# Four edits to a hybrid scan, attention and FFN kernel: an FFN input turned by DMA, norms that share a power, earlier group norms, a fifth C product on GpSimd

## The chip, the cores and the metric

The kernel runs on one NeuronCore of a Trainium2 chip. The core has five engines with an instruction queue each, worked through in order: TensorE (PE in the profile: matrix products and transposes into PSUM), VectorE (DVE), ScalarE (ACT), GpSimd (POOL), and SyncE (SP), which here only issues DMAs. They meet through semaphores. The metric is the device time of one execution in microseconds (us).

## The reference, cut to what matters

```
# layer 0, on x of (4, 64, 64, 96); L = 4096 positions, C = 96 channels, S = 16 states
xn   = layernorm(groupnorm(x), eps=1e-3) * gamma + beta
proj = xn @ W_in + b_in
value, gate, delta = proj[..., :C], sigmoid(proj[..., C:2*C]), proj[..., 2*C:3*C]
A, Bm, Cm = the rest of proj, each (B, L, C, S)
def step(h, ins):
    h_new = d * (A_t * h) + d * (B_t * u_t)
    y = g_t * sum(C_t * h_new, axis=-1)
x = x + scan(step) @ W_out + b_out
# layer 1
t = t + attention(layernorm(t, 1e-5))      # linear: q (k^T v), six heads, no softmax
t = t + ffn(layernorm(t, 1e-5))            # 96 -> 384 -> 96, inputs rounded to fp8 (5 exponent,
                                           # 2 mantissa bits), sums rounded to fp16, relu
```

The group norm has 32 groups of 3 channels and takes its mean and variance over all 4096 positions of an image.

## The kernel before

**Tiles.** Each of the 4 images is cut into 8 chunks of 512 positions, 32 chunks in all. A chunk has `NT` = 12 steps, one for each pair of a quarter of the states (4 of 16) and a third of the channels (32 of 96): 128 partitions by 512 positions. There are `K` = 384 steps.

**One step.** TensorE makes three products B, A and C, each of three matmuls over split fp32 operands (`project`, line 265). ScalarE copies B to SBUF with its bias (`b_copy`), GpSimd multiplies it by d*u (`b_mul`), VectorE multiplies A by d (`a_mul`), scans along the positions (`scan`) and multiplies C by the state (`c_mul`). In the steps whose number within the chunk is in `ON_POOL`, ScalarE copies C instead (`c_copy`) and GpSimd multiplies it (`c_mul_pool`). PSUM has two banks for A, one for B, two for C (C and D in turn) and three, M, for all the rest.

**Order.** The main loop (lines 1426 to 1448) writes the instructions step by step: in step s the B product of step s+3, the A product of s+1, the C product of s, then GpSimd's and VectorE's parts, then `call(s)`, which adds all else that is due in this step. Each engine has its own queue, so this is the order of each queue, not a time. What is due when stands in the table `AT`: a step number relative to the first step of the chunk (for the front), to the same step (for the tail of the layer 0 work), or to eight chunks later (for the FFN). So a number modulo 12 tells where in a chunk the work stands. The last steps of the FFN of image 3, and all that falls behind step 384, are ordered by the planner `Plan`.

**The front** of a chunk (class `Front`, line 681): `load_x`; group norm applied by GpSimd (`centre`, `scale`); statistics by VectorE, `rstd` by GpSimd (add eps, power -0.5, mean times -1, times r), `apply` by ScalarE; four transposes by TensorE; then d and u: `d_out` (ScalarE), `du_out` (VectorE), `write` to DRAM (`ddd`), and `read`: four DMAs that bring d and d*u back on four times as many partitions (`rep`, 1.5 MB together). `b_mul` and `a_mul` of the chunk read `rep`.

**The group norm** of an image needs sums over its 8 chunks: `load_gx` brings a chunk of x into `gx` (one buffer), TensorE transposes it (`sums`), ScalarE sums values and squares (`sums_out`). Before, the sums of image b+1 are made while image b runs, one per chunk, except that image 1's come every seven steps in image 0.

**The FFN** of a chunk (function `ffn`, line 1081): `fetch` (`xal`), `attention`, residual, statistics, `rstd`, `apply` (which writes fp8), then `transpose` (four matmuls with an identity into PSUM) and `quant_in` (ScalarE, PSUM to fp8 in SBUF: `xq`), three products `hidden0` to `hidden2`, each with three ScalarE passes, `project_f`, and the store.

**The y of a chunk** is summed over the state quarters: three DMAs by GpSimd's queue add the C products of quarters 1 to 3 to those of quarter 0 (`gather`, 768 KB each), and TensorE folds the rest.

All DMAs but the gathers and a few loads at the start come from SyncE's queue, which also works in order: a DMA that waits for its source keeps those behind it waiting.

Of the kernel before, what the change touches and what calls it, by code (L numbers as in the profile page):

```python
# [17 lines left out]
P = 128  # L18
# [22 lines left out]

    "load_x": -39, "centre": -25, "scale": -24, "stats": -22, "rstd": -22, "apply": -21,
    "transpose": -14, "affine": -13, "upper": -13, "low": -12, "proj_d": -9, "d_out": -9,
    "proj_u": -9, "du_out": -9, "write": -9, "read": -6, "proj_gate": -3, "gate_out": -1,

    "gather1": 7, "gather2": 11, "gather3": 14,

    "state_sum": 18, "gated": 18, "project_out": 19, "residual": 19, "stats_a": 20,
    "rstd_a": 21, "apply_a": 22, "transpose_a": 33, "keep": 34, "spill": 39, "gram": 24,
    "gram_out": 24, "gram_add": 26,  # L50

    "fetch": 21, "attention": 26, "residual_f": 26, "stats_f": 26, "rstd_f": 27, "apply_f": 29,
    "transpose_f": 30, "quant_in": 31, "hidden0": 37, "relu0": 37, "hidden1": 31, "relu1": 33,
    "hidden2": 38, "relu2": 38, "project_f": 40, "round_out": 40, "bias_out": 40, "total": 46,
    "store": 51,

    "sums": -31, "sums_out": -30,
}
ON_POOL = (0, 2, 7, 8)
XBUFS = 15  # L60


@with_exitstack
def conv_attn_hybrid_kernel(
# [130 lines left out]
    mhalf = const.tile([P, J], F32, name="mhalf")  # L195
    nc.gpsimd.memset(mhalf, -0.5)

# [13 lines left out]
    for r in range(2):  # L211
        t = const.tile([P, J, CA], F32, tag=f"xa{r}", name=f"xa{r}")
        nc.gpsimd.memset(t[:, :, C:CA], 1.0)
        xa_t.append(t)
        t = const.tile([CA, J, P], F32, tag=f"xal{r}", name=f"xal{r}")
        nc.gpsimd.memset(t[C:CA], 1.0)
        xal_t.append(t)

        t = const.tile([P, J, P], F8, tag=f"xn8{r}", name=f"xn8{r}")
        nc.gpsimd.memset(t, 0.0)  # L220
        xn8_t.append(t)
# [141 lines left out]

    class LayerNorm:


        def __init__(self, eps, nm):
            self.eps, self.nm, self.r = eps, nm, None

        def stats(self, src):  # L370
            st = small.tile([P, J, 6], F32, tag="st", name=f"st_{self.nm}")
            self.mv = small.tile([P, J, 2], F32, tag="mv", name=f"mv_{self.nm}")
# [5 lines left out]
        def rstd(self, shift=True):  # L378

            self.r = small.tile([P, J], F32, tag="rstd", name=f"rstd_{self.nm}")  # L380
            nc.gpsimd.tensor_scalar(self.r, self.mv[:, :, 1], self.eps, None, ALU.add)
            self.root()
            if not shift:
                return
            self.nmr = small.tile([P, J], F32, tag="nmr", name=f"nmr_{self.nm}")
            nc.gpsimd.tensor_scalar(self.nmr, self.mv[:, :, 0], -1.0, None, ALU.mult)
            nc.gpsimd.tensor_tensor(self.nmr, self.nmr, self.r, ALU.mult)

        def offset(self):

            self.r = small.tile([P, J], F32, tag="rstd", name=f"rstd_{self.nm}")
            nc.vector.tensor_scalar(self.r, self.mv[:, :, 1], self.eps, None, ALU.add)

        def root(self):
            nc.gpsimd.tensor_tensor(self.r, self.r, mhalf, ALU.pow)
# [140 lines left out]
    class GroupNorm:  # L536
# [82 lines left out]
        def root(self):  # L619
            nc.gpsimd.tensor_tensor(self.m[:, 1:2], self.v, mhalf[0:C, 0:1], ALU.pow)  # L620
# [21 lines left out]
        def spread_out(self, k0=0, k1=2):  # L642
            if k0 == 0:
                t = self.t = small.tile([P, 2, C], F32, tag="gmr", name=f"gmr_{self.b}", bufs=2)
# [3 lines left out]
    def group_norm(b, s0):  # L648
        q = {}

        def make():
            q["g"] = GroupNorm(b)
            q["g"].first()

        def call(name, *args):
            getattr(q["g"], name)(*args)

        when = [s0 + AT["sums"] + NT * n for n in range(NCH)]  # L660
        if b == 1:
            when = [8, 15, 22, 29, 36, 43, 50, 57]
        if b > 1:
            at(when[0] - 7, load_gx, b, 0)
        at(when[0] - 2, make)
        for n in range(NCH):
            if n:
                at(max(when[n] - 7, when[n - 1]), load_gx, b, n)
            at(when[n], call, "sums", n)
            at(when[n] + AT["sums_out"] - AT["sums"], call, "sums_out", n)  # L670
# [4 lines left out]
        for n, args in enumerate(chain):  # L675
            at(when[-1] + AT["sums_out"] - AT["sums"] + 1 + n, call, *args)

# [3 lines left out]
    class Front:  # L681
# [3 lines left out]
        def __init__(self, b, i):  # L685
            self.b, self.i, self.nm = b, i, f"{b}_{i}"
            self.ln = LayerNorm(1e-3, f"c_{self.nm}")
# [95 lines left out]

    def front(b, i, s0, f=None):
        if f is None:
            f = Front(b, i)
# [13 lines left out]
        late = {"centre": 0, "scale": 0, "stats": 1, "rstd": 2, "apply": 3}  # L800
# [115 lines left out]
    end.tries = 1500  # L916
# [12 lines left out]
    def tail(b, i):  # L929
# [4 lines left out]
        v, ln = {}, LayerNorm(1e-5, f"a_{nm}")  # L934
# [146 lines left out]
    def ffn(b, i, s0):  # L1081
        nm = f"{b}_{i}"
        v, ln = {}, LayerNorm(1e-5, f"f_{nm}")
# [21 lines left out]
        def apply():  # L1105

            v["xn"] = next_of(xn8_t, "xn8")
            (ln.apply_vector if vector else ln.apply)(v["xn"], t, saturate=False)

        def transpose():  # L1110
            ps = v["ps"] = bank("C" if phase["end"] else "M", [P, TC], f"xq_ps_{nm}")
# [6 lines left out]
        def quant_in():  # L1118
            v["xq"] = tile_of("xq", "h", [C, TC], F8, "xq")
# [59 lines left out]
        def store():  # L1179
# [8 lines left out]
            (("transpose_f", transpose), ("quant_in", quant_in)),  # L1188
# [17 lines left out]
        if apply in done and transpose not in done:  # L1206
# [289 lines left out]
```

## Time and profile before

| | us |
|---|---|
| median of 3 runs (1180.49 to 1182.14) | 1182.05 |
| span of the profiled execution | 1179.2 |
| TensorE busy, of the span | 1138.6 (97%) |
| VectorE busy | 1113.3 (94%) |
| GpSimd busy | 1040.1 (88%) |
| ScalarE busy | 812.9 (69%) |
| the chunks' first scans: image 0 begins | 34.8 |
| image 1 begins | 297.9 |
| the last chunk begins | 1073.3 |

The profile is of one execution, whose span lies 2.85 us below the median of the runs. TensorE's busy time is that of overlapping matmuls, whose ends are modelled: a busy TensorE isn't one at its peak. What the engines wait for is told by the rows of waits; where an engine isn't the bottleneck, its waits cost nothing. A few rows of the costliest groups (columns: line, engine, operation, output and inputs, shapes, count; then busy us, mean ns of one; then idle us before them and what ended most of it) name the operations that the change touches:

```profile
L395 POOL TENSOR_TENSOR rstd_c<-rstd_c,mhalf 128x4 f32<-128x4 f32 x32 | 33.8, 1055 | 6.5 <-DVE rstd_c L392 3.9
L386 POOL TENSOR_SCALAR nmr_c<-mv_c 128x4 f32<-128x4 f32 x31 | 7.4, 239 | 0.0
L885 POOL TENSOR_TENSOR ch<-ch,h 128x512 f32<-128x512 f32 x126 | 169.8, 1347 | 7.0 <-ACT ch L882 3.3
L876 DVE SCALAR_TENSOR_TENSOR ch<-Dps,b_bac,h 128x512 f32<-128x512 f32 x160 | 118.6, 741 | 0.4
L1120 ACT ACTIVATE xq<-xq_ps 96x512 fp8e5<-96x512 f32 x32 | 18.9, 590 | 3.6 <-PE xq_ps L1113 3.6
```

### The profile page before, as it was taken

How to read it: one execution, taken by the hardware profiler on the slowest of the kernel's cores; microseconds unless marked ns; L12 is line 12 of the kernel's file. 1: busy time of each engine (PE TensorE's matmuls, PEld its weight loads, DVE VectorE, ACT ScalarE, POOL GpSimd, SP SyncE). 2: the span in 40 equal slices, each digit the busy share in tenths (PEclk: the TensorE clock that was granted, in tenths of full speed). 3: DMA queues.
4: the chain of work that ended last, by engine and by line, in shares of the span. 5: the costliest groups of instructions: out<-in, count | busy, mean ns of one | idle time of the engine just before them, and what ended most of it. 6: DMA issues, size and time to landing. Idle time of an engine off the chain costs nothing. (4 is left out here: it accounts for less than half of the span.)

```text
span 1179.2 us, 19184 instructions
## 1 busy us (share of the span) xinstructions
PE 1138.6 (97%) x5882; PEld 874.2 (74%) x5882; DVE 1113.3 (94%) x2079; ACT 812.9 (69%) x1833; POOL 1040.1 (88%) x1187
## 2 busy tenths in 40 slices
PE   6999999999999999999999999999999999999885
PEld 5777776777777777777777777777777777777563
DVE  6999999999999999999999999999999999999865
ACT  4666655655556777777777778777777777776475
POOL 5798888888889999999999999999999999988575
PEclk8999999999999999999999999999999999999987
DMA  7676776778876777778766776776777768766221
GB/s 184 141 165 145 169 153 156 161 163 178 177 161 148 154 162 166 163 164 191 162 160 151 170 174 159 173 165 156 156 159 159 174 155 182 159 134 146 67 65 51
DMA packets 104288, 182.12 MB, mean 154 GB/s; under 512 B 42637, under 2 KB 50769, under 8 KB 104186
## 3 DMA queue, kind: packets, MB, share of 16 engines
q1 hardware_dynamic: 90060, 106.96, 37.6%
q0 software_dynamic: 13536, 73.93, 31.4%
q8 instruction: 46, 0.75, 0.3%
q14 instruction: 56, 0.46, 0.1%
q10 hardware_dynamic: 590, 0.02, 0.0%
HBM read 69.12 MB, written 24.77 MB: 80 GB/s over the span
## 5 line engine op out<-in xcount | busy, mean ns | idle before, releaser
L836 POOL TENSOR_TENSOR bu<-bu,rep 128x512 f32<-128x512 f32 x384 | 511.9, 1343 | 42.7 <-ACT state L862 32.8
L852 DVE TENSOR_TENSOR_SCAN h<-Aps,state,bu 128x512 f32<-128x512 f32 x336 | 425.9, 1268 | 0.3 <-issue 0.2
L833 ACT ACTIVATE bu<-Bps,b_bac 128x512 f32<-128x512 f32 x384 | 262.8, 684 | 198.8 <-PE Bps L269 193.1
L845 DVE SCALAR_TENSOR_TENSOR Aps<-Aps,b_bac,rep 128x512 f32<-128x512 f32 x384 | 281.6, 733 | 4.7 <-PE Aps L269 4.3
L269 PE MATMUL Bps<-xs,w 128*128 128x512 f32 x768 | 267.1, 429 | 3.8 <-ACT bu L833 3.1
L269 PE MATMUL Aps<-xs,w 128*128 128x512 f32 x768 | 241.8, 396 | 1.2 <-DVE h L852 1.0
L885 POOL TENSOR_TENSOR ch<-ch,h 128x512 f32<-128x512 f32 x126 | 169.8, 1347 | 7.0 <-ACT ch L882 3.3
L269 PEld LDWEIGHTS Aps<-xs,w 128*128 128x128 f32 x768 | 143.9, 188 | 36.9 <-DVE h L852 2.7
L269 PEld LDWEIGHTS Bps<-xs,w 128*128 128x128 f32 x768 | 126.6, 190 | 45.8 <-ACT gx_ps L577 12.6
L269 PE MATMUL Aps<-xl,w 128*128 128x512 f32 x384 | 151.8, 395 | 0.0
L269 PE MATMUL Bps<-xl,w 128*128 128x512 f32 x384 | 151.5, 395 | 0.0
L269 PE MATMUL Dps<-xs,w 128*128 128x512 f32 x384 | 120.7, 395 | 0.0
L269 PE MATMUL Cps<-xs,w 128*128 128x512 f32 x384 | 120.6, 395 | 0.0
L876 DVE SCALAR_TENSOR_TENSOR ch<-Dps,b_bac,h 128x512 f32<-128x512 f32 x160 | 118.6, 741 | 0.4
L891 POOL DMA_DIRECT2D ch<-ch x94 | 88.9, 946 | 1.4 <-DMA ch<-ch 1.1
L269 PEld LDWEIGHTS Bps<-xl,w 128*128 128x128 f32 x384 | 72.3, 188 | 17.5
L269 PEld LDWEIGHTS Aps<-xl,w 128*128 128x128 f32 x384 | 72.1, 188 | 17.6
L269 PEld LDWEIGHTS Dps<-xs,w 128*128 128x128 f32 x384 | 72.1, 188 | 17.5
L269 PEld LDWEIGHTS Cps<-xs,w 128*128 128x128 f32 x384 | 72.1, 188 | 17.5
L882 ACT ACTIVATE ch<-Cps,b_bac 128x512 f32<-128x512 f32 x94 | 64.5, 686 | 24.2 <-PE Cps L269 24.2
L269 PE MATMUL Cps<-xl,w 128*128 128x512 f32 x192 | 75.8, 395 | 0.0
L269 PE MATMUL Dps<-xl,w 128*128 128x512 f32 x192 | 75.6, 394 | 0.0
(200 smaller groups left out, 2049.4 us busy)
## 6 DMA issues: line engine op xcount, KB each, us to landing
ch<-ch POOLq DMA_DIRECT2D x94, 768.0 KB, 6.7
rep<-ddd SPq DMA_DIRECT2D x124, 384.0 KB, 7.5
ddd<-dd SPq DMA_DIRECT2D x31, 384.0 KB, 3.2
xl<-lo SPq DMA_DIRECT2D x62, 128.0 KB, 2.4
x<-in_x_dram SPq DMA_DIRECT2D x32, 192.0 KB, 2.9
xatd<-xat SPq DMA_DIRECT2D x32, 192.0 KB, 3.6
xal<-xatd SPq DMA_DIRECT2D x32, 192.0 KB, 5.4
out_dram<-o SPq DMA_DIRECT2D x32, 192.0 KB, 2.5
```

Source lines behind the costliest of these rows:

```text
L269: nc.tensor.matmul(ps, lhsT=wt[:, n], rhs=mv, start=(n == 0), stop=(n == 2))
L833: nc.scalar.activation(self.bu, self.b_ps, AF.Identity, bias=self.bias(0))
L836: nc.gpsimd.tensor_tensor(self.bu, self.bu, rep[self.b, self.i][:, 1, self.cg], ALU.mult)
L845: nc.vector.scalar_tensor_tensor(self.a_ps, self.a_ps, self.bias(1), rep[self.b, self.i][:, 0, self.cg], ALU.add, ALU.mult,)
L852: nc.vector.tensor_tensor_scan(self.h, self.a_ps, self.bu, 0.0 if self.i == 0 else state[self.sh, self.cg], ALU.mult, ALU.add,)
L876: nc.vector.scalar_tensor_tensor(self.slot(), self.c_ps, self.bias(2), self.h, ALU.add, ALU.mult)
L882: nc.scalar.activation(self.ch, self.c_ps, AF.Identity, bias=self.bias(2))
L885: nc.gpsimd.tensor_tensor(self.ch, self.ch, self.h, ALU.mult)
L891: nc.gpsimd.dma_start(chs[g, 0], chs.pop((g, sh)), accum_op=ALU.add)
```

## The change

Four edits and a new table of steps:

- **The FFN's input** is turned by a DMA in 22 of 32 chunks. `apply` writes its fp8 values into the high byte of 2-byte cells (`xn8` is now fp16, 128 by 4 by 128), SyncE issues a transposing DMA of these cells into `xq`, and the `hidden` products read `xq` as fp16, in which such a cell has the same value. The four transposing matmuls and `quant_in` stay only in the ten chunks that the planner orders at the end.
- **Norms share a power.** Norms due in the same step put their means and variances into one tile (class `Roots`), and GpSimd takes power -0.5 of all at once. In the new table the convolution's norm (step -19) and the FFN's (29) fall on the same step of a chunk; the attention's (21) stays alone. The adds and the multiplication by -1 become tensor-tensor operations with constant tiles.
- **All group norms early.** The sums of images 1, 2 and 3 are made in steps 8 to 107, at steps given by `GN_AT`, and `gx` is loaded up to four steps ahead.
- **`ON_POOL`** has five steps instead of four.

```diff
 AT = {
-    "load_x": -39, "centre": -25, "scale": -24, "stats": -22, "rstd": -22, "apply": -21,
-    "transpose": -14, "affine": -13, "upper": -13, "low": -12, "proj_d": -9, "d_out": -9,
-    "proj_u": -9, "du_out": -9, "write": -9, "read": -6, "proj_gate": -3, "gate_out": -1,
-    "gather1": 7, "gather2": 11, "gather3": 14,
...
-    "fetch": 21, "attention": 26, "residual_f": 26, "stats_f": 26, "rstd_f": 27, "apply_f": 29,
-    "transpose_f": 30, "quant_in": 31, "hidden0": 37, "relu0": 37, "hidden1": 31, "relu1": 33,
-    "hidden2": 38, "relu2": 38, "project_f": 40, "round_out": 40, "bias_out": 40, "total": 46,
-    "store": 51,
+    "load_x": -33, "centre": -25, "scale": -24, "stats": -20, "rstd": -19, "apply": -18,
+    "transpose": -14, "affine": -13, "upper": -13, "low": -13, "proj_d": -9, "d_out": -9,
+    "proj_u": -8, "du_out": -7, "write": -7, "read": -7, "proj_gate": -4, "gate_out": -4,
+    "gather1": 6, "gather2": 10, "gather3": 13, "state_sum": 18, "gated": 18, "project_out": 19,
+    "residual": 19, "stats_a": 20, "rstd_a": 21, "apply_a": 22, "transpose_a": 34, "keep": 35,
+    "spill": 35, "gram": 24, "gram_out": 25, "gram_add": 28, "fetch": 19, "attention": 24,
+    "residual_f": 24, "stats_f": 27, "rstd_f": 29, "apply_f": 31, "turn_f": 31, "hidden0": 34,
+    "relu0": 37, "hidden1": 33, "relu1": 33, "hidden2": 38, "relu2": 41, "project_f": 42,
+    "round_out": 43, "bias_out": 47, "total": 50, "store": 55, "sums": -31, "sums_out": -30,
 }
-ON_POOL = (0, 2, 7, 8)
+GN_AT = {
+    1: [8, 16, 23, 29, 36, 41, 47, 57],
+    2: [12, 20, 27, 31, 39, 43, 53, 59],
+    3: [65, 68, 76, 80, 90, 95, 100, 107],
+}
+GX_AHEAD = 4
+ON_POOL = (0, 2, 3, 5, 8)
...
-        t = const.tile([P, J, P], F8, tag=f"xn8{r}", name=f"xn8{r}")
+        t = const.tile([P, J, P], F16, tag=f"xn8{r}", name=f"xn8{r}")
...
+    class Roots:
+        def root(self):
+            if self.done:
+                return
+            self.done = True
...
+                nc.gpsimd.tensor_tensor(
+                    self.r[:, k:m], self.mv[:, k:m, :, 1], eps_t[ln.eps][:, 0 : m - k], ALU.add
+                )
+            nc.gpsimd.tensor_tensor(self.r, self.r, mhalf[:, 0:n], ALU.pow)
+            nc.gpsimd.tensor_tensor(self.nmr, self.mv[:, :, :, 0], minus[:, 0:n], ALU.mult)
+            nc.gpsimd.tensor_tensor(self.nmr, self.nmr, self.r, ALU.mult)
...
+        order = sorted((s, b, n) for b, steps_of in place.items() for n, s in enumerate(steps_of))
+        for k, (s, b, n) in enumerate(order):
+            if k:
+                at(max(s - GX_AHEAD, order[k - 1][0]), load_gx, b, n)
+            if n == 0:
+                at(s - 2, make, b)
+            at(s, call, b, "sums", n)
+            at(s + 1, call, b, "sums_out", n)
...
-            (ln.apply_vector if vector else ln.apply)(v["xn"], t, saturate=False)
+            cells = v["xn"].bitcast(F8).rearrange("p j (c k) -> p j c k", k=2)[:, :, :, 1]
+            (ln.apply_vector if vector else ln.apply)(cells, t, saturate=False)
+
+        def turn():
+            v["xq"] = sb("xq", [P, J, P], F16, f"xq_{nm}")
+            nc.sync.dma_start(
+                v["xq"], v["xn"].rearrange("p j c -> p (j c)"), transpose=True
+            )
+            v["xq"] = v["xq"][0:C].rearrange("c j p -> c (j p)")
...
-            (("transpose_f", transpose), ("quant_in", quant_in)),
+            (("turn_f", turn),),
```

In the queues this gives, per chunk of images 1 to 3, on SyncE: `x`, `ddd`, four `rep`, the store of an output, the transposing DMA, `xal`, three copies of the split, `xatd`. Before it was `ddd`, the store, `xatd`, four `rep`, `x`, `xal`, `gx`, three copies.

## The prediction

> **What bounds the kernel now.** I read the page's slices first, then busy time by stage, then VectorE's timeline over one chunk, then SyncE's timeline with the DMA share, because one part of the change adds a transfer that TensorE waits for. Busy time by stage (columns: stretch, its us, each engine's busy us, granted clock, DMA share, GB/s):
>
> ```profile
> 34.80:297.90 263.10, 257.66 (x1220) 197.77 (x1219) 255.57 (x422) 157.78 (x377) 229.16 (x243) 1.00 0.72 158
> 297.90:1073.30 775.40, 774.98 (x4024) 598.01 (x4023) 757.38 (x1400) 575.62 (x1306) 721.36 (x816) 1.00 0.74 163
> 1104.30:1179.20 74.90, 53.83 (x382) 38.09 (x373) 45.80 (x156) 45.48 (x93) 45.52 (x63) 0.84 0.21 59
> ```
>
> The first row is image 0 (8 chunks, 32.9 us each), the second the 23 chunks from image 1's start to the last chunk's (33.7 us each), the third the tail, which the change hardly touches. TensorE, VectorE and GpSimd are all above 93% in the second; ScalarE, at 74%, has room. VectorE in image 3:
>
> ```profile
> 804.83 1.28 DVE L852 TENSOR_TENSOR_SCAN h<-Aps,state,bu 128x512 f32<-128x512 f32 x1
> 806.02 0.74 DVE L845 SCALAR_TENSOR_TENSOR Aps<-Aps,b_bac,rep 128x512 f32<-128x512 f32 x1
> ...
> 809.10 0.73 DVE L876 SCALAR_TENSOR_TENSOR ch<-Dps,b_bac,h 128x512 f32<-128x512 f32 x1
> 809.76 1.27 DVE L852 TENSOR_TENSOR_SCAN h<-Aps,state,bu 128x512 f32<-128x512 f32 x1
> ```
>
> No idle time stands in it, and start follows start: 1.19 us for a scan, 0.66 for a product. The next chunk's first scan starts at 838.22, 33.4 us later, so VectorE's order sets the pace. TensorE is close behind: in the timeline a block of three products takes 0.70 us (Aps starts at 503.74, Cps at 504.44), three blocks 2.1 us a step, 25.2 us a chunk. Start to start in the same view the small ones add, per chunk: the d, u and gate products 2.1, the state sum 1.0, output and attention 0.8 each, gram 0.6, two transposes 0.7, the FFN 1.3 (of it 0.3 for transposing its input): 7.3. TensorE's own work is about 32.5 us. Neither engine can lose much.
>
> SyncE's queue around the replication of d and d*u:
>
> ```profile
> 578.91 0.32 SPq L769 DMA_DIRECT2D ddd<-dd  x1
> 579.27 0.45 SPq L1180 DMA_DIRECT2D out_dram<-o  x1
> 579.77 0.90 SPq L961 DMA_DIRECT2D xatd<-xat  x1
> 582.22 1.75 SPq L776 DMA_DIRECT2D rep<-ddd  x4
> ...
> 584.00:586.00 2.00, 2.00 (x15) 0.89 (x13) 2.00 (x3) 1.80 (x6) 2.00 (x3) 1.00 1.05 257
> 586.00:588.00 2.00, 2.00 (x11) 1.49 (x9) 1.82 (x3) 0.79 (x3) 1.76 (x3) 1.00 1.07 221
> 588.00:590.00 2.00, 2.00 (x14) 1.64 (x13) 1.03 (x3) 1.15 (x2) 1.89 (x2) 1.00 1.10 223
> ```
>
> `rep` waits 3.3 us for `ddd` to land, and then its 1.5 MB fill all 16 DMA engines until about 590. What is issued behind it waits:
>
> ```profile
> 248.48 2.51 SPq L776 DMA_DIRECT2D rep<-ddd  x4
> 251.03 0.44 SPq L125 DMA_DIRECT2D x<-in_x_dram  x1
> 251.57 1.15 SPq L130 DMA_DIRECT2D gx<-in_x_dram  x1
> ...
> DMA to landing us min/median/max: 4.8/7.2/11.4
> ```
>
> The maximum is this `gx`: 192 KB took 11.4 us to land, against 2.9 us for an `x` load of the same size on a quiet queue.
>
> [...] No run here shows one; I price its 128 KB at 225 GB/s (windows above), 0.6 us, as an estimate.
>
> **The change part by part.**
>
> *Five C products on GpSimd.* VectorE loses one 0.66 us product per chunk: 33.4 becomes 32.8 us. ScalarE gains a copy of 0.69 us and loses `quant_in` (0.59): even. GpSimd gains 1.25 us (start to start of its products).
>
> *One power for two norms.* Of three chains add, power, times -1, times r, two (convolution and FFN norm, both at step 5 modulo 12) merge. A chain costs 0.24+1.05+0.24+0.20 = 1.7 us and about 1.87 with gaps, three 5.6. An 8-column power isn't in the trace. Below: as 4 columns, 1.05; above: twice, 2.1. The one-column power (651 ns for 96x1) and four columns (1050) give 0.13 us a column, so I take 1.6. The chains then cost about 4.2 us, and GpSimd ends at -0.15 us per chunk (between -0.7 and +0.35). It stays under 32.8.
>
> *Group norms in the first image.* 16 sums (four 128x128 transposes each, about 0.36 us of TensorE; 1.6 us of ScalarE) leave images 1 and 2 for image 0, where no FFN runs. TensorE there has 2.2 us less work per chunk than later, so 0.7 us more fits, and ScalarE is at 60%. Loads of `gx` four steps ahead mostly avoid the time of `rep`. Worth up to 0.5 us in 16 chunks where TensorE is nearly the bound; image 0, with its lost product, I put at -2 us in all.
>
> *The transposing DMA.* It removes four FFN transposes (0.3 us of TensorE) and `quant_in`, in 22 chunks; the ten in the tail keep them. The hidden products now stream fp16 instead of fp8, which the trace doesn't have; with the same 512 columns I give them the same time (if they took as long as three of the split products, 0.2 us each more, TensorE would lose 0.6 us a chunk). It adds a wait: `hidden1`, on TensorE at step 33, waits for a DMA issued at step 31, and behind `hidden1` stand all of TensorE's products. In SyncE's new order it comes after `ddd`, the four `rep` and an output store. And `du_out` moves from step 3 to 5 modulo 12, so `rep` goes two steps later: just ahead of the transpose.
>
> Count from T0, the end of `du_out`, which is the start of scan 6 (583.7 in the chunk shown). `rep` is issued at T0+3.3, its fourth 1.3 us later, and with the page's median of 7.5 us to landing it lands at T0+12.1. The store (192 KB) and the transpose (128 KB) follow, 1.4 us at the same rate: T0+13.5. The first gather also moves, from step 7 to 6, and will share the engines with `rep`; I add 0.8 us (0 if it doesn't, 3 if all its 768 KB go first). The transpose lands at about T0+14.3.
>
> TensorE reaches `hidden1` in the middle of step 9 (its other per-chunk products stand half a step behind VectorE in the same way: the gram's copy, of step 24, that is 0, runs at 0.9 in the trace). Step 6 is on VectorE a scan, a product with A, one with C and the gating (1.19+0.64+0.66+0.6), step 7 the same with the residual for the gating, step 8 a scan, a product with A and the statistics (2.8); with half of step 9 that makes 3.1+3.0+2.8+1.2, so T0+10.1. It stands for 4 us, and behind it the blocks B, A and C of the next steps. ScalarE waits with it (the copies of `relu1` need `h_ps`), and VectorE as soon as it has used up A, of which two banks exist. From `hidden1` to the next `du_out`, TensorE has seven steps of 2.1 us, 1.4 us of the eighth and 3.9 us of small products (two transposes 0.7, gram 0.6, attention 0.8, two hidden products 0.3, d and u 1.4), 20.0 in all; then VectorE has a product with A and `du_out` itself, 1.3. That is 21.3, so the period becomes 14.3+21.3 = 35.6 us, against 33.7: of the 4 us, 1.2 go into VectorE's lost product and TensorE's lead, and the FFN transposes that are gone. Break-even is a landing at T0+12.4. Nothing makes the loss good later in the chunk: TensorE, with 32.2 us of work, has no idle time to catch up in.
>
> *`rep` itself later.* GpSimd's first product with it starts at 595.99, 12.3 us after 583.7, about when it lands (T0+12.1). That product ends some 3.2 us before its scan (597.3 against 600.5). A delay below this costs nothing alone; in the forecast it lies beside TensorE's stall.
>
> *Sum.* 21 periods with the stall, 1.9 us each: +40. Image 0: -2; the two chunks of image 1 before the first stall: -1.5. The span goes from 1179.2 to 1215.7. The median of the runs is 2.85 above the span; I keep this: 1218.5 us. A measurement tells about 0.2%, 2.4 us, from no change.
>
> **Rivals.**
>
> *The transpose lands in time.* [...] against: the 11.4 us. Then VectorE's 32.8 us rule from image 1 on: 23 chunks times 0.9 is -21, with image 0 -23: 1159 us. This is the case on the other side, decided by a landing before about T0+11.5; from T0+12.4 the stall eats the gain.
>
> *It breaks even.* A landing near T0+12.5 gives 33.8 us: about 1180. It asks for 1.8 us less than I count: with no gather in the way (0.8), and another 1 us saved on store or transpose.
>
> *The gather goes ahead of `rep`.* With 3 us instead of 0.8, the landing is at T0+16.5, the period 37.8, the sum 21 times 4.1 less 3.5: +83, 1264 us. For it: the gather's earlier step. Against: it waits for products of the steps before, and in the chunk shown goes out at 586.85, after `rep`.
>
> *The shared power costs more than it saves.* At the upper bound GpSimd needs some 32.3 us, still under VectorE's 32.8. It moves nothing by itself.
>
> **How the numbers follow.** The forecast's own case, 1195 to 1235, has 0.48; in time or nearly (1150 to 1179) 0.29; break-even (within 0.2%) 0.04; between it and 1195, 0.05; above 1235, 0.14. So faster 0.29, same 0.04, slower 0.67. The range that leaves out no more than 2 in 10 runs from 1157 to 1252. The likeliest case alone: 1195 to 1235.
>
> **What would show it.** Right: a wait of `h_ps` on TensorE for the DMA of `xq`, 3 to 5 us, some 21 times; `xq`'s median to landing above 7 us; steps 9 and 10 of a chunk longer than before, with VectorE idle before a product with `Aps`; VectorE's busy share falling from 94%. Wrong: `xq` lands within 5 us of its issue, or TensorE shows no such wait; then the period is about 32.8 us. If in image 0 TensorE waits for `gx`, the step of the group norms was wrong. An 8-column power near 2.1 us, or GpSimd without idle time, would show the third step wrong.

## The result, and the profile after

| | before | after |
|---|---|---|
| median, us | 1182.05 (1180.49 to 1183.79) | 1381.60 (1376.86 to 1392.44) |
| ratio to before, 95% interval | | 1.169 (1.165 to 1.174) |
| span of the profiled execution, us | 1179.2 | 1390.7 |
| image 0, first scan to first scan of image 1 | 263.0 | 283.2 |
| chunks 8 and 9 | 64.4 | 74.0 |
| 21 periods, chunk 10 to the last | 711.1 (33.9 each) | 893.3 (42.5 each) |
| from the last chunk's first scan to the end | 105.9 | 105.2 |

The profile after is of the slowest of the five runs, 10.8 us above their median, so its stages add up to more than the medians differ by. Its span is 211.5 us longer than before: 182.3 of them in the 21 periods in which a transposed input is used, 20.2 in image 0, where no FFN runs, and 9.6 in the two chunks between.

The page of the kernel after says it in its head (busy time and share of each engine) and in the chain that ended last, where a DMA now stands with 6% of the span; the last two lines are the `rep` of the pages before and after, from the lists of DMA issues:

```profile
PE 1184.8 (85%) x5797; PEld 913.1 (66%) x5797; DVE 1111.9 (80%) x2049; ACT 817.9 (59%) x1841; POOL 1055.8 (76%) x1166
...
PE 19%; DMA 6%; DVE 2%; POOL 1%; ACT 1%; issue 1%; SPq 0%; DVEq 0%; ACTq 0%; POOLq 0%
...
rep<-ddd SPq DMA_DIRECT2D x124, 384.0 KB, 7.5
rep<-ddd SPq DMA_DIRECT2D x124, 384.0 KB, 9.7
```

Busy times of VectorE and GpSimd are within 2% of those before; it is idle time that was added. TensorE's busy time grew by 46 us with 85 matmuls fewer; why is told below. The median `rep` takes 9.7 us from issue to landing, against 7.5. The list of waits (us in total, times, longest):

```profile
DVE Aps L883 <- PE Aps L275: 200.6, 57, 9.0
ACT h L1178 <- PE h_ps L1170: 169.9, 21, 9.0
...
PE h_ps L1170 <- DMA xq<-xn: 153.3, 21, 8.1
POOL bu L874 <- DMA rep<-ddd: 102.1, 27, 5.2
```

The line of `xq` is the cause of the first two: 21 times TensorE stood at `hidden1`, 7.3 us on average, and VectorE and ScalarE stood for TensorE. One of them, from the start of SyncE's queue to the end of the stand. SyncE's issues (start, us, operation):

```profile
578.34 0.32 SPq L806 DMA_DIRECT2D ddd<-dd  x1
581.40 1.82 SPq L813 DMA_DIRECT2D rep<-ddd  x4
583.27 1.86 SPq L1226 DMA_DIRECT2D out_dram<-o  x1
585.24 3.77 SPq L1151 DMA_TRANSPOSE xq<-xn  x1
```

the gather that GpSimd issues, from its own timeline:

```profile
581.38 0.92 POOL L929 DMA_DIRECT2D ch<-ch  x1 [0.30 <-POOL ch L923]
```

and TensorE's timeline at `hidden1`:

```profile
587.98 0.39 PE L275 MATMUL Dps<-xl,w 128*128 128x512 f32 x1
596.21 0.59 PE L1170 MATMUL h_ps<-xq,w_q 96*128 96x512 f16 x1 [7.84 <-DMA xq<-xn]
596.24 1.41 PE L275 MATMUL Bps<-xs,w 128*128 128x512 f32 x2
597.45 0.63 PE L275 MATMUL Bps<-xl,w 128*128 128x512 f32 x1
```

T0, the end of `du_out`, is 578.3. The gather (768 KB) is issued 0.02 us before `rep` and shares the engines with it: in the packet records its packets run from 584 to 590, and `rep`'s last packet ends at 594.4, 13.0 us after the issue (before, 7.6 in the chunk that the prediction shows). The store and the transpose behind it run from 593 to 596. TensorE reaches `hidden1` at 588.4 and stands until 596.2. Afterwards a matmul takes up to 0.63 us where it took 0.39 before the stand.

### The profile page after: what moved, and what is told of

Read it like the earlier page. It is cut to its first block, busy times and chain, and to the rows that moved or that the text cites. A ratio compares the mean times of both kernels' runs of the same rounds, so it can differ in the third digit from the quotient of the medians.

```text
span 1390.7 us, 19063 instructions
## 1 busy us (share of the span) xinstructions
PE 1184.8 (85%) x5797; PEld 913.1 (66%) x5797; DVE 1111.9 (80%) x2049; ACT 817.9 (59%) x1841; POOL 1055.8 (76%) x1166
## 5 line engine op out<-in xcount | busy, mean ns | idle before, releaser
L874 POOL TENSOR_TENSOR bu<-bu,rep 128x512 f32<-128x512 f32 x384 | 522.5, 1406 | 207.2 <-DMA rep<-ddd 102.1
L275 PE MATMUL Bps<-xs,w 128*128 128x512 f32 x768 | 277.7, 444 | 0.4 <-ACT bu L871 0.2
L275 PEld LDWEIGHTS Bps<-xs,w 128*128 128x128 f32 x768 | 139.3, 197 | 197.6 <-issue 165.4
L275 PE MATMUL Aps<-xs,w 128*128 128x512 f32 x768 | 252.9, 411 | 9.2 <-DVE h L890 8.5
L923 POOL TENSOR_TENSOR ch<-ch,h 128x512 f32<-128x512 f32 x156 | 212.2, 1360 | 51.7 <-ACT ch L920 48.3
L1170 PE MATMUL h_ps<-xq,w_q 96*128 96x512 f16 (+1 forms) x96 | 41.4, 457 | 155.3 <-DMA xq<-xn 153.3
L1178 ACT CAST h<-h_ps 128x512 f16<-128x512 f32 x63 | 36.9, 586 | 169.9 <-PE h_ps L1170 169.9
L275 PE MATMUL Cps<-xs,w 128*128 128x512 f32 x384 | 128.1, 416 | 0.0
L914 DVE SCALAR_TENSOR_TENSOR ch<-Dps,b_bac,h 128x512 f32<-128x512 f32 x130 | 96.5, 742 | 0.9 <-PE Dps L275 0.5
L914 DVE SCALAR_TENSOR_TENSOR ch<-Cps,b_bac,h 128x512 f32<-128x512 f32 x98 | 72.8, 743 | 7.4 <-PE Cps L275 7.0
```

Of the source, the lines that this page charges most:

```text
L275: nc.tensor.matmul(ps, lhsT=wt[:, n], rhs=mv, start=(n == 0), stop=(n == 2))
L874: nc.gpsimd.tensor_tensor(self.bu, self.bu, rep[self.b, self.i][:, 1, self.cg], ALU.mult)
L914: nc.vector.scalar_tensor_tensor(self.slot(), self.c_ps, self.bias(2), self.h, ALU.add, ALU.mult)
L923: nc.gpsimd.tensor_tensor(self.ch, self.ch, self.h, ALU.mult)
L1170: nc.tensor.matmul(v["h", m], lhsT=w1_q[:, m * P : (m + 1) * P], rhs=v["xq"], start=True, stop=True)
L1178: nc.scalar.copy(h16, v["h", m])
```

## The experiments

Each changes the kernel after, unless it says otherwise. Ratios, with their 95% intervals, are to runs of the kernel before on the same chip. Its median there was 1180.6 to 1183.3 us, so differences of a few us between experiments on different chips are not told apart. "Image 0" and "chunks 8 to 31" are the differences of first scans; before they are 263.0 and 775.5 us.

### Where the wait for the transpose comes from

**e1_du_early** puts `rep` back by two steps, ahead of the transpose by more. Theory 'queue' is that `xq` came late because of `rep`: SyncE issues `rep` ahead of it, `rep` shares the engines with the gather (its packets run from 582.4 to 594.4 in the chunk above), and those of `xq` run only from 593.9 to 595.5.

```diff
-"proj_u": -8, "du_out": -7, "write": -7, "read": -7,
+"proj_u": -9, "du_out": -9, "write": -9, "read": -6,
```

> The changed kernel with one thing undone: u's product, du_out, the write of ddd and the read of rep at the steps of the kernel before (-9, -9, -9, -6 instead of -8, -7, -7, -7). Theory 'queue' [...]: rep goes out two steps earlier, ahead of the gather, xq lands about when TensorE comes to hidden1; the wait of h_ps for xq falls from 153 us to under 30, the time from 1382 to 1160-1200. Rival 'transpose itself' (a transposing DMA takes some 10 us from issue to landing wherever it stands): the wait stays above 100 us and the time above 1300.

1238.6 us, ratio 1.049 (1.047 to 1.051). The waits, to be set beside those of the kernel after:

```profile
DVE dd L772 <- ACT dd L768: 31.0, 30, 1.4
...
PE h_ps L1170 <- DMA xq<-xn: 27.1, 21, 3.1
```

The wait for `xq` falls from 153.3 to 27.1 us, its landing from 10.7 to 5.9 us, and image 0 goes from 283.2 to 269.9. The mechanism is confirmed, the time isn't: 1200 at most was expected, and a wait that was not there before, VectorE at `du_out` for ScalarE's copy of d, is in the list.

**e2_hidden_late** leaves `rep` where it is and reads `xq` later; **e3_pe_turn** takes the transposing DMA out and turns the input on TensorE again, in the new table.

```diff
# e2
-"hidden0": 34, "relu0": 37, "hidden1": 33, "relu1": 33,
+"hidden0": 37, "relu0": 37, "hidden1": 36, "relu1": 36,
# e3, with the turn of the kernel before
-"turn_f": 31,
+"transpose_f": 32, "quant_in": 32,
```

> The changed kernel with the three hidden products and their relus three steps (hidden0 and hidden1) later: hidden1 36, hidden0 37, hidden2 38. Theory 'queue': xq is there in time, the 153 us of waiting go, and what is left over the kernel before is what rep's lateness costs GpSimd (image 0 lost 20 us without any xq): 1190-1230. Rival 'a late rep is the real limit' (xq only waits beside it): the wait moves to GpSimd's product with rep, and the time stays above 1300.

> The changed kernel with the FFN input turned by TensorE and ScalarE again (steps 32 and 32, ahead of hidden1 at 33) in all chunks; shared powers, early group norms, five C products and all other steps stay. Theory 'queue': no wait for a DMA at hidden1; time as in the run with hidden late, within 15 us: 1190-1230, image 0 as slow as in the changed kernel (283 us). Rival 'the other three edits lose by themselves': above 1300.

1242.0 us (1.051; 1.046 to 1.056) and 1239.5 us (1.048; 1.043 to 1.053). In e2 `xq` still takes 10.6 us to land, but TensorE waits for it only 9.0 us in all. So three quite different ways of removing the same wait give the same 1240: it is worth about 140 of the 199 us (medians), and the DMA in itself costs nothing that e3 saves. Both expected less; some 60 us are made elsewhere.

The two traces tell more on the transpose. In e2 and e3, where TensorE doesn't stand there, the first gather, at the same step, goes out 6.1 us after T0 (median from chunk 10 on) instead of 3.1, behind `rep`'s first packets, and `rep`'s last packet then ends at T0+12.0, not T0+15.5. But `xq` doesn't land earlier for it. In e2, with T0 at 587.67:

```profile
593.68 0.92 POOL L929 DMA_DIRECT2D ch<-ch  x1 [0.30 <-POOL ch L923]
...
DMA to landing us min/median/max: 10.1/10.6/11.2
```

Here the packet records have the gather from T0+12.1 to T0+16.4, some 195 KB in a us in packets of 6144 bytes, and from T0+13 to T0+15 the transpose beside it with 8 KB in a us in packets of 256 bytes: about 32 packets of each in a us. About 100 of its 128 KB move only as the gather ends, and its last packet comes 0.4 us after the gather's. In the medians `xq`'s last packet ends at T0+17.2 in e2, against T0+16.7 in the kernel after, and at T0+17.2 in e6 below, where the gather goes ahead of `rep`. In these three, with the gather ahead of, amid or behind `rep`, `xq`'s last packet ends within 0.5 us of the same place.

**e4_gather_late** tries to take the gather out of `rep`'s way with the smallest edit.

```diff
-"gather1": 6, "gather2": 10, "gather3": 13,
+"gather1": 7, "gather2": 11, "gather3": 14,
```

> The changed kernel with the three gathers at the steps of the kernel before (7, 11, 14 instead of 6, 10, 13). Theory 'queue' with the gather as the part that was sized too small: the gather goes out after rep, rep's last packet comes 7.5-9 us after its issue instead of 12-13, xq lands some 4 us earlier: the wait falls from 153 to 60-100 us and the time to 1240-1310. Rival 'rep and xq fill the engines by themselves': the wait stays above 130 us.

1374.3 us, a miss: TensorE still waited 145 us for `xq`. In the trace the gather is now issued mostly 0.7 to 1.1 us after `rep` instead of with it, and `rep` still takes 12.0 us. While TensorE stands, GpSimd has little to do and runs up to the gather early (T0+3.95 here, T0+6.5 with the same step in e5 below, where TensorE doesn't stand): a step number doesn't fix a time. Nor would a gather behind `rep` have been enough: in e5 `xq`'s last packet still ends at T0+17.4.

### What the other edits cost

**e5_late_both** is e2 with e4's gathers; **e6_four_products** is e2 with four C products.

```diff
# e5, besides e2's edit
-"gather1": 6, "gather2": 10, "gather3": 13,
+"gather1": 7, "gather2": 11, "gather3": 14,
# e6, besides e2's edit
-ON_POOL = (0, 2, 3, 5, 8)
+ON_POOL = (0, 2, 7, 8)
```

> The changed kernel with its hidden products three steps later (as in e2_hidden_late) and, besides, the three gathers at the earlier kernel's steps 7, 11 and 14. In e2_hidden_late GpSimd stood 62 us in 26 places for one gather before it issued the next, because the first gather of a chunk is issued beside rep and took about 11 us to land. Theory (GpSimd is the bound there, 32 us of instructions a chunk and about 2.5 us of standing for a gather): with the gathers one step later the first one starts behind part of rep, lands sooner after its issue, the wait falls under 20 us and the period goes from 35.2 to about 33.7, time 1195 to 1215. Rival (what is left of the loss is made elsewhere, in the order of the front or of the norms): wait or no wait, the time stays between 1230 and 1250.

> e2_hidden_late with four C products on GpSimd, at steps 0, 2, 7 and 8 as before the change. Theory (GpSimd with five products is too full, 1.25 us a chunk): the period falls by about 1.2 us or more in all 31 chunks, time 1195 to 1210. Rival (VectorE is as near its bound as GpSimd): VectorE gets 0.66 us more a chunk and the time stays between 1230 and 1255. Either way image 0, where no FFN runs and no transposing DMA is issued, shows it alone: 281.8 us with five products, below 275 by the theory.

e5: 1228.1 (1.036; 1.030 to 1.041), 14 us better than e2 and between what its two theories expected. GpSimd's wait for the earlier gather fell only from 62 to 50 us (under 20 was expected), so that wait isn't shown to be the reason; image 0 got longer (288.1 after 281.8). e6: 1280.7 (1.082; 1.079 to 1.086), slower, which neither theory expected. With two products instead of four in the steps ahead of it, the first gather is issued ahead of `rep`: in the packet records `rep` begins to move 4.3 us (median of 31) after its issue instead of 0.96, and the list of waits of e6 has

```profile
POOL bu L874 <- DMA rep<-ddd: 121.5, 24, 6.8
...
DVE Aps L883 <- DMA rep<-ddd: 51.9, 22, 4.5
```

So in the new table a GpSimd that comes to the gather sooner makes `rep` later. That says nothing on what the fifth product costs.

**e7_old_table** puts the edits into the table of before, with the transpose at step 30 (and output steps as after).

> The changed kernel with the step table of before (front, norms, attention, gathers, FFN norm), the transposing DMA at step 30 behind apply at 29, and the hidden products at 36 to 38; output steps as in the changed kernel. Five C products and the group norms of the first image stay; no two norms share a power, since no two fall on one step. If the new table (with the shared power and the rep two steps later) is what costs the 60 us left in e2_hidden_late: 1175 to 1200, image 0 about 262. If the five products or the early group norms cost them: 1230 to 1250, image 0 about 280.

1372.4 us: a new trap. Image 0 takes 271.3, but then TensorE stands at the attention (its wait, SyncE's wait at the load of x, and SyncE's issues in one chunk):

```profile
PE a_ps L1144 <- DMA xal<-xatd: 120.8, 18, 7.4
...
SPq L133 <- POOL gram L1028: 370.9, 15, 25.3
...
737.26 0.58 SPq L1234 DMA_DIRECT2D out_dram<-o  x1
762.23 0.40 SPq L133 DMA_DIRECT2D x<-in_x_dram  x1
762.67 0.59 SPq L1139 DMA_DIRECT2D xal<-xatd  x1
```

SyncE stands some 24 us a chunk at the load of x for GpSimd, and `xal` is issued right behind that load (steps -39 and 21, both 9 modulo 12). The load waits for a buffer that `total` frees, and with the output steps of after `total` comes four steps later, at step 50: the trap of e17 below. (The gram's addition, which the list names, is GpSimd's at the same step of a chunk, 2 modulo 12.) It was not tested by itself, but e11 and e15, which have `total` at 46 and `fetch` at 19, show no such wait. The run doesn't answer its question.

Then the single edits, each alone in the kernel before: **e8_five_alone**, **e11_turn_alone**, **e12_gn_alone**.

```diff
# e8
-ON_POOL = (0, 2, 7, 8)
+ON_POOL = (0, 2, 3, 5, 8)
# e11: apply and turn as in the change, and
-"fetch": 21, "transpose_f": 30, "quant_in": 31, "hidden0": 37, "relu0": 37, "hidden1": 31, "relu1": 33,
+"fetch": 19, "turn_f": 32, "hidden0": 37, "relu0": 37, "hidden1": 36, "relu1": 36,
# e12: group_norms(GN_AT) as in the change, instead of
-        if b + 1 < B:
-            group_norm(b + 1, b * NCH * NT)
```

> The kernel before with one line changed: C products at steps 0, 2, 3, 5 and 8 on GpSimd instead of 0, 2, 7 and 8. The prediction's sum gives VectorE 0.66 us less and GpSimd 1.25 us more a chunk; GpSimd then stands at about 33 us of 33.9. If GpSimd has the room: 1165 to 1185. If GpSimd becomes the bound through its waits (gather, nmr for ScalarE): 1200 to 1230, with ScalarE waiting for nmr.

> The kernel before with the transposing DMA alone: FFN input in 2-byte cells, turned at step 32, its products hidden1 and hidden0 at 36 and 37, fetch at 19 so that SyncE issues it ahead of the transpose. Four C products, group norms and table as before otherwise. TensorE loses about 0.3 us and ScalarE 0.59 us a chunk in 22 chunks. If this was the edit worth making and only its place was wrong: 1170 to 1180, no wait for xq above 1 us. If its 4 us of issue on SyncE delay fetch, spill or rep, or the wait remains: 1190 to 1250, and the wait list names xal, xq or rep. e7_old_table had the transpose ahead of fetch and lost 1372.

> The kernel before with the group norms alone moved: the 24 sums of images 1 to 3 at the changed kernel's steps 8 to 107, each gx load four steps ahead. The prediction took 0.5 us in 16 chunks as a gain (8 us) and nothing lost in image 0. If so: 1172 to 1178, image 0 263 to 265, images 1 and 2 about 4 us shorter each. If the loads of gx and the extra 16 sums are paid in image 0: image 0 266 to 275, images 1 and 2 shorter by at most as much, 1178 to 1190.

| alone | us | ratio | image 0 | chunks 8 to 31 |
|---|---|---|---|---|
| five products | 1193.9 | 1.009 (1.006 to 1.012) | 268.1 | 782.9 |
| transposing DMA, well placed | 1188.1 | 1.005 (1.003 to 1.006) | 263.0 | 782.1 |
| early group norms | 1180.3 | 0.998 (0.997 to 0.999) | 267.8 | 769.5 |

The fifth product costs 10.7 us, more than "has the room" and less than "bound through its waits" allowed. The transposing DMA, never waited for, still costs 6: TensorE's waits show no `xq`, and the 0.3 us a chunk that it saves TensorE bring no gain. The run also moves `fetch` and the hidden products, so that the 6 us are the DMA's own isn't shown. The early group norms are the one edit that pays, and it ends 0.2% under the kernel before, so it is the one version run here that is faster than both. Its profile is of the fastest of its 22 runs, 3.4 us under the median, so the windows flatter it a little. Its windows by image (as in the prediction: stretch, its us, busy us of TensorE, its weight loads, VectorE, ScalarE, GpSimd, clock, DMA share, GB/s) show both sides of it, image 0 first:

```profile
34.40:302.20 267.80, 262.26 (x1272) 202.69 (x1271) 257.85 (x426) 171.79 (x423) 230.59 (x248) 1.00 0.74 163
302.20:568.20 266.00, 265.23 (x1350) 204.75 (x1349) 262.02 (x480) 185.92 (x423) 246.71 (x280) 1.00 0.74 162
```

Image 0 has 52 matmuls more than the 1220 before and takes 4.8 us longer; image 1 has 25 fewer than before and takes 2.7 less.

**e9_three_moves** combines e1, e2 and e4. **e10_no_share** is e9 with no power shared.

```diff
# e10, besides e9's edits
-"rstd": -19,
+"rstd": -20,
-MV_BUFS = {1: 3, 2: 2, 3: 2}
+MV_BUFS = {1: 4, 2: 2, 3: 2}
```

> The changed kernel with three groups of steps moved together: du_out back to -9 with write and read (rep issued two steps earlier), gathers back at 7, 11 and 14, hidden products at 36 to 38. The transposing DMA, five C products, the shared power and the group norms of the first image stay. Image 0, where no FFN runs, took 263 us before the change, 283 after, 270 in e1_du_early and 268 with the five products alone, so rep's lateness is 13 us of image 0's 20. Theory (rep late is the next cost behind the wait for xq): image 0 268 to 272, TensorE's wait for xq under 15 us in all, chunks 8 to 31 under 795 us, time 1180 to 1205. Rival (the order of front and norms in the new table costs most of the rest): chunks 8 to 31 above 810, time above 1215.

> e9_three_moves with rstd of the convolution norm one step earlier (-20 instead of -19), so that it shares no power with the FFN norm: three powers of 4 columns a chunk (1.03 us each) instead of one of 8 (1.66) and one of 4. If sharing gains what the prediction took (0.15 us or more a chunk on a GpSimd that is nearly the bound): 4 to 25 us slower than e9. If sharing costs, since ScalarE stands for nmr_c at the convolution norm's apply (44 to 53 us in e2 and e3): 5 to 30 us faster than e9, and that wait below 15 us. No effect: within 4 us of e9.

1226.2 us (1.038; 1.035 to 1.040) and 1236.4 (1.046; 1.044 to 1.048). The three moves bring 155 of the 199 us; image 0 is as expected (271.3), the rest is not: the rival was right. With sharing it is 10 us faster there, though e10 also has this norm's `rstd` a step earlier, so the 10 aren't the power's alone. ScalarE does stand for `nmr_c` longer (22.1 us in e9, 5.6 in e10), and e9 is the faster all the same. The rows of the powers in the kernel after:

```profile
L401 POOL TENSOR_TENSOR rstd_c<-rstd_c,mhalf 128x8 f32<-128x8 f32 x20 | 33.3, 1663 | 1.6
L401 POOL TENSOR_TENSOR rstd_a<-rstd_a,mhalf 128x4 f32<-128x4 f32 x32 | 33.0, 1031 | 2.5
```

### Edits or table?

**e13_gn_share**, **e14_gn_share_five** and **e15_all_old_table** add one edit at a time in the table of before: early group norms and shared power; with five products; with the transposing DMA too.

```diff
# e13, against the table of before, besides class Roots and group_norms(GN_AT)
-"rstd": -22, "apply": -21,
+"rstd": -21, "apply": -20,
# e14, besides
-ON_POOL = (0, 2, 7, 8)
+ON_POOL = (0, 2, 3, 5, 8)
# e15, besides: turn and the steps of e11
```

> The kernel before's table and turn on TensorE, four C products at 0, 2, 7 and 8, with the group norms of the first image and the shared power: rstd of the convolution norm at -21 instead of -22 and apply at -20, so that it falls on the FFN norm's step (27, both 3 modulo 12). e12_gn_alone without the sharing took 1180.3. If sharing is worth what e9 and e10 differ by (10 us): 1166 to 1174. If it is worth only where GpSimd is overfull (five products): 1177 to 1184. If the later nmr_f or the longer power delays ScalarE: above 1184.

> e13_gn_share with five C products on GpSimd (0, 2, 3, 5, 8). Alone the fifth product cost 10.7 us, with GpSimd 1.25 us a chunk fuller. The shared power takes 0.75 us a chunk back. If the loss was GpSimd's fullness: at most 4 us above e13. If it is the place of the products (steps 3 and 5, which VectorE and ScalarE wait for): again about 10 us above e13.

> All four edits in the earlier kernel's order of steps: e14_gn_share_five with the transposing DMA at step 32, fetch at 19 and the hidden products at 36 and 37 as in e11_turn_alone. By the single edits (five products +10.7, turn +5.9, group norms -1.9, sharing 0 to -10): 1187 to 1197, against 1226 for e9_three_moves, which has the same four edits in the new table. So about 30 to 40 us of the loss is the new table's order of the other steps if this comes out below 1200; if the edits hurt each other instead, it comes out at 1215 or more and the table is not to blame.

1187.2 (1.006; 1.004 to 1.007), 1184.2 (1.003; 1.001 to 1.004) and 1187.4 (1.005; 1.004 to 1.007). With four products, sharing (and `rstd` and `apply` a step later) loses 7 us against e12. With the norms shared, the fifth product, 10.7 us alone, costs nothing (e14 is 3 us under e13). And all four edits together, in the old order, cost 5 us: 39 less than e9, which has the same edits. The rest of the loss is the order of the other steps.

**e16_norm_rows** and **e17_output_rows** put parts of the new table into e15.

```diff
# e16
-"load_x": -39, "stats": -22, "rstd": -21, "apply": -20, "low": -12, "proj_gate": -3, "gate_out": -1,
-"attention": 26, "residual_f": 26, "stats_f": 26, "rstd_f": 27, "apply_f": 29,
+"load_x": -33, "stats": -20, "rstd": -19, "apply": -18, "low": -13, "proj_gate": -4, "gate_out": -4,
+"attention": 24, "residual_f": 24, "stats_f": 27, "rstd_f": 29, "apply_f": 31,
# e17
-"gram_out": 24, "gram_add": 26, "relu2": 38, "project_f": 40, "round_out": 40, "bias_out": 40, "total": 46, "store": 51,
+"gram_out": 25, "gram_add": 28, "relu2": 41, "project_f": 42, "round_out": 43, "bias_out": 47, "total": 50, "store": 55,
```

> e15_all_old_table with the new table's steps of the front and of the FFN norm alone (load_x -33, stats -20, rstd -19, apply -18, low -13, proj_gate and gate_out -4, attention and residual_f 24, stats_f 27, rstd_f 29, apply_f 31). e9_three_moves, with all of the new table but rep, gathers and hidden products, is 39 us above e15. In e9 VectorE stood 1.35 us a chunk for the d copy of ScalarE ahead of du_out, which the trace of e15 shows with 0.15, and stats_f is now issued on that same step. If these rows carry the 39 us: 1215 to 1228, that wait back above 1 us a chunk. If not: 1185 to 1195.

> e15_all_old_table with the new table's output and gram steps alone (relu2 41, project_f 42, round_out 43, bias_out 47, total 50, store 55, gram_out 25, gram_add 28). If these rows carry the 39 us between e15 and e9: 1215 to 1228. If not: 1183 to 1195. Both e16 and e17 below 1200 would mean that only the two together cost it.

e16: 1211.5 (1.025; 1.022 to 1.028), 24 of the 39 us, with VectorE's wait at `du_out` back (36.7 us; 31.0 in e1, 37.0 in e9). e17: 1306.6, a pairing that says nothing on the question: SyncE stands 381 us (194 in e15) at the load of x (step -39) for `total`, which is now four steps later and frees the buffer, and everything on SyncE stands behind it.

**e18_stats_ahead** takes one wait out of e9. VectorE's timeline in e9, at `du_out`:

```profile
664.20 1.28 DVE L890 TENSOR_TENSOR_SCAN h<-Aps,state,bu 128x512 f32<-128x512 f32 x1
666.01 0.76 DVE L883 SCALAR_TENSOR_TENSOR Aps<-Aps,b_bac,rep 128x512 f32<-128x512 f32 x1 [0.52 <-PE Aps L275]
668.15 0.75 DVE L772 SCALAR_TENSOR_TENSOR dd<-dug_ps,b_dug,dd 96x512 f32<-96x512 f32 x1 [1.38 <-ACT dd L768]
668.82 0.73 DVE L423 BATCH_NORM_STATS2 st_f<-x 128x6 f32<-128x96 f32 x4
```

`du_out` stands 1.38 us for ScalarE's copy of d, and the statistics that could be done meanwhile are queued behind it.

```diff
-"stats": -20, "stats_f": 27,
+"stats": -22, "stats_f": 26,
```

> e9_three_moves with the statistics of both norms back on step 2 modulo 12 (stats -22, stats_f 26 instead of -20 and 27). In e9 VectorE stood 1.35 us a chunk at du_out for ScalarE's copy of d: in the earlier order the two statistics stand ahead of du_out and cover the product of d and that copy, in e9 they stand behind it. 31 chunks of 1.35 us are 42 us. If that is what e9 still loses: that stand falls below 0.4 us a chunk and the time to 1185 to 1200. If it is only a symptom of another wait: the stand may go, and the time stays above 1215.

1187.4 us (1.005; 1.003 to 1.007). The same place in e18:

```profile
645.50 0.73 DVE L423 BATCH_NORM_STATS2 st_c<-z 128x6 f32<-128x96 f32 x4
646.14 0.37 DVE L425 BATCH_NORM_AGGREGATE mv_c<-st_c 128x2 f32<-128x6 f32 x4
646.42 0.71 DVE L423 BATCH_NORM_STATS2 st_f<-x 128x6 f32<-128x96 f32 x4
647.05 0.36 DVE L425 BATCH_NORM_AGGREGATE mv_c<-st_f 128x2 f32<-128x6 f32 x4
647.33 1.25 DVE L890 TENSOR_TENSOR_SCAN h<-Aps,state,bu 128x512 f32<-128x512 f32 x1
648.49 0.73 DVE L883 SCALAR_TENSOR_TENSOR Aps<-Aps,b_bac,rep 128x512 f32<-128x512 f32 x1
649.66 0.75 DVE L772 SCALAR_TENSOR_TENSOR dd<-dug_ps,b_dug,dd 96x512 f32<-96x512 f32 x1 [0.43 <-ACT dd L768]
```

Some 1.8 us of statistics lie ahead of `du_out` and cover the product of d and its copy; the stand is 0.43 us. In all it falls from 37.0 to 12.8 us, and TensorE, which in e9 was idle 27.0 us ahead of A products until a scan freed the bank, stands so for 2.3. VectorE's idle time, over the 31 periods from the first chunk to the last, goes from 2.53 to 1.32 us a chunk. That is some 37 of the 40 us by which these periods get shorter. The loss then divides like this: 1381.6 after; 155 us for the three moves (e9); 39 for the statistics (e18); 5 for the four edits with what is left of the new table. Why the rows of e16 gave 24 us in the old table and the statistics alone 39 in the new one was not worked out.

## Why the prediction was wrong

**The bound and the mechanism** held: TensorE stood at `hidden1` 21 times for `xq`, VectorE then for `Aps`, and TensorE arrives there at T0+10.1 (median of 21), as forecast to the tenth.

**"The first gather also moves ... I add 0.8 us (0 if it doesn't, 3 if all its 768 KB go first)"** is the step that failed. `xq` was there at T0+17.4 (median of the 21), not T0+14.3, and the gather's share is what was missed. In the chunk above `rep`'s last packet ended at T0+16.1, where the sum without a gather has T0+12.1: 4.0 us. Store and transpose took 1.8 us more (1.4 taken; that a transposing DMA moves its 128 KB at the rate of an ordinary one was the author's estimate). But `rep` is only where the cost shows in this order: in e2 the gather runs behind `rep`, the same cost falls on the transpose, and its last packet ends no sooner. In each of the three places seen (after, e2, e6) the gather's 768 KB moved before `xq` was done. At e2's 195 KB in a us they take 3.9 us, an estimate, and 12.1 + 3.9 + 1.4 is 17.4. The forecast treated it as a matter of which goes first. Its reason against the rival with the gather ahead (T0+16.5, 1264 us) compared 586.85, the gather's issue in the trace of before, with the `rep` of before, issued at 582.22. In the new order, by the forecast's own T0 of 583.7, `rep` goes out at T0+3.3 and that gather stands at T0+3.15, beside it. In the trace of the kernel after the gather's packets run amid `rep`'s from 584 to 590 and `rep` takes 5.4 us longer than its 7.6 before, and in e2 the transpose moved 8 KB in a us in packets of 256 bytes beside the gather's 195 KB in packets of 6144.

**"From `hidden1` to the next `du_out` ... 21.3"** measured 24.6 us (596.2 to 620.8). Some 1.6 of the 3.3 us are a slower TensorE: in the windows of the kernel after, the 7.8 us of the stand and the 3.8 us that follow it have clocks of 0.77 and 0.58,

```profile
588.40:596.20 7.80, 0.00 (x0) 0.00 (x0) 2.38 (x3) 0.00 (x0) 3.31 (x7) 0.77 1.07 209
596.20:600.00 3.80, 3.79 (x11) 2.92 (x11) 0.60 (x1) 3.10 (x7) 1.41 (x3) 0.58 0.65 129
```

and 3.8 times 0.42 is 1.6, an estimate from these clocks that takes TensorE's pace to follow them. The trace's clock record shows the same at every one of the 21 stands: the clock falls to 0.5 for 6.83 or 10.24 us, beginning 2.1 to 4.3 us after the stand did, which by the same estimate costs 1.5 to 3.0 us once TensorE works again, 2.2 on average and 47 in all. In the kernel before, between the same chunks, it stays at 1.00. This is also about the 46 us by which TensorE's busy time grew. What sets the start and the length of a fall was not shown. The prediction counted a stall at its own length. With the clock's loss taken off, 22.9 us are left in nearly every period, 1.6 more than forecast; these were not resolved. Of a stand of 4.2 us the forecast let 1.9 reach the period, and named 1.2 of the 2.3 that were to be made good; a stand of 7.3 us on average made the period 8.6 longer. (Its small products add to 3.8, not 3.9, which changes nothing.) Together: 17.9 + 24.6 = 42.5 us a period against 35.6, in 21 periods 145 of the 163 us missed.

**"A delay below this costs nothing alone"**, of the later `rep`, was wrong. In image 0, where nothing waits for `xq`, putting it back (e1) took the image from 283.2 to 269.9 us. That is 13 of the 20 us image 0 lost, where the prediction had -2. The move also takes `rep` out of the gather's way, so how much is lateness and how much the gather isn't told apart.

**The five products** were priced as 0.66 us a chunk gained; alone they cost 10.7 us in all, and nothing with the shared power (e14 against e13). So the sum of GpSimd's work, which left room, didn't tell its cost; which wait it works through was not traced. **The shared power**'s price (1.6 us) was right at 1.66. "It moves nothing by itself" looks wrong both ways: +7 us with four products (e13 against e12), -10 with five (e9 against e10), but each of these pairs also moves the norm's `rstd` by a step. **The early group norms** gained about what was said in images 1 to 3 (6.0 us against up to 8, in the profile of its fastest run) but cost 4.8 in image 0, where the forecast, with the fifth product, had -2; that product alone cost 5.1 there.

**The order of the rest** was taken as neutral: the prediction has no term for moving the statistics from step 2 to steps 3 and 4 of the chunk. e16 and e18 show what they were there for. The change put `du_out` behind them again, on step 5, so it kept their cover and paid with a `rep` two steps later; with `du_out` back in its place and the statistics not, VectorE pays at `du_out` instead.

That the sign was right rests on the one wait. Its size was lost in the gather's share, in the clock after the stand, and in a table of steps that was taken as neutral.

## What to carry to other kernels

Where a new wait sits behind a DMA, count in full every transfer that will be in flight before its last packet, those of other engines' queues too. Here a gather of 768 KB on another queue cost the transpose about 4 us, ahead of it or beside it (3.9 us at the 195 KB in a us of e2, an estimate): beside it the transpose, in packets of 256 bytes, moved 8 KB in a us. Place these transfers by the new order, and not by where they stood in the trace before. A step number in a hand-written order is not a time (the same gather went out at T0+3.1 and T0+6.1), and each small instruction ahead of a dependent one may be its cover, so when it is moved ask which wait it hid. Count the clock after a stall of TensorE, too: here each stand of 5.9 to 8.1 us was followed by work at a clock of 0.5, which cost some 2.2 us more on average, an estimate from the clock record.

## What was not expected of the hardware

- The issue of a transposing DMA of 128 KB occupied SyncE for 4.0 us (median of 22) in the kernel after, 1.3 in e2 and 2.0 in e1, while an ordinary one took 0.3 to 2.0 in the kernel after; why it differs was not found. From issue to landing: 5.9 us in e1, 7.6 in e18, 10.7 in the kernel after. In the records it moves in packets of 256 bytes.
- GpSimd's power on 8 columns took 1.66 us, on 4 columns 1.03: about 0.16 us a column and 0.40 fixed, an estimate from these two (it gives 0.56 for one column, where 0.65 was measured).
- Beside a gather that moved 195 KB in a us in packets of 6144 bytes, a transposing DMA moved 8 KB in a us in packets of 256 bytes, about 32 packets of each, and most of the rest as the gather ended (e2).
- At each of 21 stands of 5.9 to 8.1 us TensorE's clock fell to half, for 6.83 or 10.24 us, 2.1 to 4.3 us after the stand began (the kernel after).
- Where the gather from GpSimd's queue was issued ahead of `rep` (e6), `rep`'s first packet came about 4.3 us after the issue (median of 31), against 0.96 in the kernel after.
